# A third query buffer for a sparse graph-attention kernel, with its scatter, its tail and a table load moved

## The chip, the cores and the metric

The kernel runs on one core of a Trainium2 chip. The metric is the device time of one execution in microseconds. Six things work beside each other on the core: TensorE (matrix products; its weight loads are shown as a row of their own, PEld), VectorE (DVE), ScalarE (ACT), GpSimd (POOL, which here mostly issues indirect transfers), SyncE (SP, which issues plain transfers) and sixteen DMA engines.

## What is computed

The reference is one layer of graph attention over 3327 nodes with 1024 features, all in float32. Each node has few neighbours: an adjacency entry is set with a chance of 0.24%, made symmetric, and each node is its own neighbour.

```python
h = jnp.maximum(_layernorm(x, axis=-1), 0.0)
f = h @ Wf + bf
g = h @ Wg + bg
e = jax.nn.relu(f @ g.T)
scores = jnp.where(adj > 0, e, NEG)
attention = jax.nn.softmax(scores, axis=1)
x_W = h @ W + bW
x = x + attention @ x_W
```

Here `adj` is 3327 x 3327 and the three weights are 1024 x 1024.

## The kernel before

The kernel works on the edges only (`edge_path`); a dense path lies behind a branch that is taken only if a node has too many neighbours.

Two identities save most of the work. The score of an edge is h_i A h_j with A = Wf Wg^T, so that one vector q = h_i A per node suffices and no g is made. And the attention is summed over rows of h, y_i = sum of p_ij h_j, before it goes once through W.

**Part one**, to about 258 us, streams the adjacency matrix in 26 tiles of 128 rows, finds the column numbers of each row's edges, normalises x into `hd` in DRAM, makes A on TensorE, and sorts the nodes by degree. Each of 26 tiles of sorted nodes then has a fixed number of slots (`CAPS`, L27), 37 for the tile of the highest degrees and 11 for the last.

**Part two** runs over the tiles in the order `ORDER = [24, 0, 1, ... 23, 25]` (L29). The change is all in this part. For one tile s with cap slots:

- `fetch` (L733): GpSimd gathers the tile's edge lists (`pi`) and its own rows of h (into a buffer of the pool `G`).
- `prepare` (L748): TensorE transposes these rows (L703), ScalarE copies them to `hT` (L704), and TensorE makes q in three chunks of 342 columns, 24 products (L764). `prepared` (L786) and `emptied` (L776) copy the chunks from PSUM to the tile `q` (L780) and refill the emptied bank with the row that the next product adds to (L727).
- `dot` (L817): for each slot, GpSimd gathers 128 rows of 4 KB into a G buffer (L691), and VectorE takes their dot products with q (L824).
- `softmax` (L849): small operations on VectorE, one exponential on ScalarE (L860). Tiles of more than 16 slots are worked in two units, with the rescaling of an online softmax between them; smaller tiles are one unit. There are 15 tiles of two units in ORDER's middle (0 to 14).
- `combine` (L893): the weighted sum of the slots. `on_tensor` (L875) says which slots of the last unit TensorE adds: ScalarE scales such a row (L904) and TensorE adds it transposed into PSUM (L887, eight products a slot). The other slots are added by VectorE (L910) into the first row `y`, which ScalarE has scaled (L908). TensorE gets cap - 12 slots, in the last two tiles of ORDER cap - 7.
- `project` (L912): TensorE adds y transposed (L887), ScalarE copies the sum to `yT` (L918), TensorE multiplies it with W (L924, 16 products).
- `result` (L931): ScalarE copies the product out (L942), and GpSimd gathers the rows of x onto it with an accumulating transfer. `finish` (L951): GpSimd scatters the rows to `out` (L954).

The main loop (L1003) goes over the units. In the last unit of tile s it fetches and prepares the tile two places on, so that q is made two tiles ahead, and it holds two q. In front of the weighted sum, `AHEAD` = 3 dots of the next unit are placed. The scatter of an earlier result is placed in the next unit that comes, and has to wait there for the accumulating gather.

A scheduler orders the instructions of each engine at build time; `in_line` (L712) keeps the order of the products of TensorE and the copies of ScalarE as the program has it. Each engine then runs its own instructions in that fixed order. The pool `G` has 26 buffers; a gather waits for a free one.

Of the kernel before, what the change touches and what calls it, by code (L numbers as in the profile page):

```python
# [8 lines left out]
FP = mybir.dt.float32  # L9
I32 = mybir.dt.int32  # L10
AF = mybir.ActivationFunctionType
# [15 lines left out]
CAPS = [37, 25, 23, 22, 21, 21, 20, 20, 19, 19, 18, 18, 17, 17, 17, 16, 16, 15, 15, 15, 14, 14, 13, 13, 12, 11]  # L27

ORDER = [24, *range(24), 25]  # L29
ONE_CHUNK = 16  # L30
FIRST = 10
LARGEST = 16
AHEAD = 3
LAG = 4


# [259 lines left out]
def edge_path(ctx: ExitStack, tc: tile.TileContext, x, adj, Wf, bf, Wg, bg, W, bW, out, flag):  # L296
# [376 lines left out]

    bWb = ctx.enter_context(tc.tile_pool(name="bW", bufs=1)).tile([P, O], FP, name="bWb")
    nc.sync.dma_start(bWb, bW[None, :].to_broadcast([P, O]))
    psp = ctx.enter_context(tc.tile_pool(name="ps", bufs=3))
    gpool = ctx.enter_context(tc.tile_pool(name="G", bufs=26))
    mpool = ctx.enter_context(tc.tile_pool(name="more", bufs=1))
    qpool = ctx.enter_context(tc.tile_pool(name="q", bufs=2))
    hTpool = ctx.enter_context(tc.tile_pool(name="hT", bufs=1))  # L680
    yTpool = ctx.enter_context(tc.tile_pool(name="yT", bufs=1))
    xpool = ctx.enter_context(tc.tile_pool(name="xp", bufs=2))
    jpool = ctx.enter_context(tc.tile_pool(name="junk", bufs=1))
    small = ctx.enter_context(tc.tile_pool(name="small", bufs=2))
    p_q = ctx.enter_context(tc.tile_pool(name="p_q", bufs=2, space=PSUM))
    p_t = ctx.enter_context(tc.tile_pool(name="p_t", bufs=2, space=PSUM))
    p_y = ctx.enter_context(tc.tile_pool(name="p_y", bufs=1, space=PSUM))
# [33 lines left out]
    def filled(pool, name, row, w, at):  # L721
        ps = pool.tile([P, CB], FP, name=name)
        if at < 2:
            nc.tensor.matmul(ps, ident, A_sb[:, 0, :CB], start=True, stop=True)
        o = at * w % row.shape[1]
        banks[name, at] = ps
        return nc.scalar.copy(ps[:, :w], row[:, o : o + w])  # L727

    for at in range(2):
        filled(p_q, "ps_q", vb, QB, at)  # L730
# [2 lines left out]
    def fetch(s):  # L733

        if s == ORDER[1]:

            with tc.issue_after(st["gathered"].ins):
                return fetched(s)
        fetched(s)
# [8 lines left out]
    def prepare(s):  # L748
        e = st[s]
        pi = e["pi"]  # L750
        hT = hTpool.tile([P, KD, P], FP, name="hT")
        with in_line():
            copied, ins = transposed2(hT, e["hp"])
        if queue:
            queue["act"], queue["pe"] = copied, ins
        e["q"] = qpool.tile([P, QW], FP, name="q")
        e["ps_q"] = []
        for i, o in enumerate(range(0, QW, QB)):
            at = 3 * ORDER.index(s) + i
            ps = banks.pop(("ps_q", at))  # L760
            e["ps_q"].append(ps)
            with in_line():
                for k in range(KD):
                    ins = nc.tensor.matmul(  # L764
                        ps[:, :QB], hT[:, k, :], A_sb[:, k, o : o + QB], start=False, stop=(k == KD - 1),
                        skip_group_check=True,
                    )
            if queue:
                queue["pe"] = ins

            if not i:
                emptied(s, i)
        if not queue:
            prepared(s)
# [11 lines left out]
    def prepared(s):  # L786

        e = st[s]
        pi = e["pi"]
        emptied(s, 1)  # L790
        emptied(s, 2)
        df = pi.bitcast(FP)[:, KL : KL + 1]
        mask = e["mask"] = small.tile([P, KM], FP, name="mask")
        nc.vector.tensor_scalar(mask, iotak, df, NEG, op0=ALU.is_ge, op1=ALU.mult)
        e["sc"] = small.tile([P, KM], FP, name="sc")
        if s == NT - 1:
            e["x"] = gpool.tile([P, O], FP, name="G")
            gather(e["x"], x[:, :], perm[:, s : s + 1])
        e["edges"] = [pi[:, k : k + 1] for k in range(KL)]
        if s >= MORE:  # L800
            return

        ct = xpool.tile([P, O], FP, name="res")[:, : SEG * 8]
        with tc.issue_after(st["gathered"].ins):
            gather(ct, cd[:, :], perm[:, s : s + 1])
        found = mpool.tile([P, KM - KL + 8], FP, name="found")
        for i in range(0, KM - KL + 8, 8):
            nc.vector.max(found[:, i : i + 8], ct)
            if i < KM - KL:
                nc.vector.match_replace(ct, found[:, i : i + 8], ct, 0.0)  # L810
        more = mpool.tile([P, KM - KL], I32, name="more")
        nc.vector.tensor_scalar(more, found[:, 8:], 1.0, -1.0, op0=ALU.max, op1=ALU.add)
        e["edges"] += [more[:, k : k + 1] for k in range(KM - KL)]
# [61 lines left out]
    def on_tensor(s, k0, k1):  # L875


        m = min(max(0, CAPS[s] - (7 if s in ORDER[-2:] else 12)), k1 - k0 - 2) if s != ORDER[0] else (k1 - k0) // 2
        ks = range(max(k0, 1), k1)
        return [k for i, k in enumerate(ks) if (i + 1) * m // len(ks) > i * m // len(ks)]  # L880

# [11 lines left out]
    def combine(s, k0, k1, last):  # L893
        e = st[s]
        if not k0:
            e["y"] = G[s, 0]
        y = e["y"]
        e["first"] = True
        pe = on_tensor(s, k0, k1) if last else []
        for k in range(k0, k1):  # L900
            p = e["sc"][:, k : k + 1]
            g = G[s, k]
            if k in pe:
                queue["act"] = nc.scalar.activation(g, g, AF.Copy, scale=p)  # L904
                queue["pe"] = sum_transposed(e, g, e["first"], False)
                e["first"] = False
            elif k == 0:
                queue["act"] = nc.scalar.activation(y, y, AF.Copy, scale=p)  # L908
            else:
                e["summed"] = nc.vector.scalar_tensor_tensor(y, g, p, y, op0=ALU.mult, op1=ALU.add)  # L910
# [89 lines left out]


    rest, done_with = None, []
    for i, (s, k0, k1) in enumerate(units):  # L1003
        last = k1 == CAPS[s]
        at = ORDER.index(s)
        if last and at + 2 < NT:
            fetch(ORDER[at + 2])
        dots(s, range(k0, k1))
        softmax(s, k0, k1, last)
        if i + 1 < len(units):  # L1010
            s2, a, b = units[i + 1]
            dots(s2, range(a, min(b, a + AHEAD)))
        if done_with:
            finish(done_with.pop())
        combine(s, k0, k1, last)
        if rest:
            rest()
            rest = None
        if last:
            if at:  # L1020
                result(ORDER[at - 1])
                done_with.append(ORDER[at - 1])
            if at + 2 < NT:
                prepare(ORDER[at + 2])

            def rest(s=s, at=at):
                if at + 2 < NT:
                    prepared(ORDER[at + 2])
                project(s)

            if not at or i + 1 == len(units) or units[i + 1][2] == CAPS[units[i + 1][0]]:
                rest()
                rest = None
            if at + 2 == NT - 1:
                bad = failed()
# [43 lines left out]
```

## Time and profile before

| | |
|---|---|
| time, median of 3 | 1349.98 us (1345.41 to 1358.32) |
| profiled run | 1346.38 us, span 1344.7 us |
| TensorE busy | 1118.3 us, 83% |
| VectorE busy | 1166.1 us, 87% |
| ScalarE busy | 598.4 us, 44% |
| GpSimd busy | 901.1 us, 67% |
| data moved | 374.46 MB, mean 278 GB/s |
| GpSimd waiting in front of scatters for the gather of x | 66.4 us, 20 waits |
| ScalarE loads of an activation table | 3, 1283 ns each |

The profile is one execution on the chip. Busy time of an engine is what its instructions took; a wait is put down to the engine or transfer that came last. The chain of waits is followed back from the last instruction to what released each step, so it names what set the end. A table of stretches gives the same busy times for parts of the span, which is needed here because the limits change along it: about 258 us of part one, then tile 24 and the large tile 0 until 391 us, and then 25 tiles of falling size, at 31 to 55 us each.

### The profile page before, as it was taken

The page shows a single profiled execution, that of the slowest core. Times are in us where ns is not written, and L with a number is a line of the kernel's source. Part 1 is how long each engine was busy: PE and PEld are TensorE (multiplying, and loading weights), DVE is VectorE, ACT ScalarE, POOL GpSimd, SP SyncE. Part 2 cuts the span into 40 slices and gives each one's busy share as a digit, 9 for nine tenths or more (in the row PEclk, how much of TensorE's full clock was granted, in tenths as well). Part 3 has the DMA queues.
Part 4 walks back from the last instruction along what each step waited for, and adds up shares of the span by engine and source line. Part 5 has one row for each costly group of instructions (what it writes and reads, how often), then busy time and mean ns, then how long its engine had stood idle before and what let it go on. Part 6 is the DMA issues. An engine that isn't in the chain of part 4 may idle for free.

```text
span 1344.7 us, 14333 instructions
## 1 busy us (share of the span) xinstructions
PE 1118.3 (83%) x4448; PEld 707.6 (53%) x4448; DVE 1166.1 (87%) x2360; ACT 598.4 (44%) x940; POOL 901.1 (67%) x678
## 2 busy tenths in 40 slices
PE   2588896288339678989998999998999999999996
PEld 2355554155136546555565655555555555555553
DVE  4789899668978898999998999998988999999880
ACT  6779687223043534544354444433343333333250
POOL 6699889275566677677776666666665776766711
PEclk9989898598769899999998999999999999999998
DMA  9999996687569788898988879888786998888831
GB/s 355 336 381 348 385 382 206 249 306 270 169 201 315 249 285 304 275 307 288 309 298 299 281 279 309 308 292 298 235 278 210 295 288 284 284 272 265 293 100 50
DMA packets 101660, 374.46 MB, mean 278 GB/s; under 512 B 14731, under 2 KB 18474, under 8 KB 98247
## 3 DMA queue, kind: packets, MB, share of 16 engines
q0 software_dynamic: 79584, 286.77, 64.0%
q1 hardware_dynamic: 11004, 71.01, 13.7%
q10 hardware_dynamic: 10986, 15.67, 3.3%
q8 instruction: 37, 0.61, 0.2%
q14 instruction: 49, 0.40, 0.1%
HBM read 344.11 MB, written 29.30 MB: 278 GB/s over the span
## 4 chain that ended last, share of the span: by engine, by line
PE 46%; DVE 16%; issue 11%; ACT 10%; DMA 9%; POOL 6%; another core or an unknown queue 0%; ACTq 0%; POOLq 0%; SPq 0%; DVEq 0%
PE ps_o L924 19%; PE ps_q L764 17%; PE yT_ps L887 7%; ACT G L904 5%; DVE G L910 5%; DVE cand L478 4%; DMA G<-hd,pi 3%; DVE junk L824 3%; POOL G L691 3%; PE ps_A L554 2%; POOL r L427 2%; DMA r<-in_adj_dram 1%; ACT r L420 1%; DMA cd<-cand 1%; DMA hd<-xt 1%
## 5 line engine op out<-in xcount | busy, mean ns | idle before, releaser
L691 POOL DMA_INDIRECT G<-hd,pi x454 | 539.7, 1189 | 203.7 <-issue 109.5
L824 DVE CUSTOM_DVE_ANT_0 junk<-G,q 128x1024 bf16<-128x1024 f32 x456 | 584.9, 1283 | 58.2 <-DMA G<-hd,pi 30.5
L924 PE MATMUL ps_o<-W_sb,yT 128*128 128x512 f32 x832 | 370.3, 603 | 24.3 <-ACT yT L918 13.7
L764 PE MATMUL ps_q<-A_sb,hT 128*128 128x342 f32 x1248 | 371.5, 457 | 18.2 <-ACT hT L704 15.2
L910 DVE SCALAR_TENSOR_TENSOR G<-G,sc 128x1024 f32<-128x1024 f32 x279 | 357.8, 1282 | 14.1 <-ACT G L908 11.6
L764 PEld LDWEIGHTS ps_q<-A_sb,hT 128*128 128x128 f32 x1248 | 236.8, 192 | 144.8 <-ACT hT L704 20.6
L924 PEld LDWEIGHTS ps_o<-W_sb,yT 128*128 128x128 f32 x832 | 157.4, 192 | 221.8 <-issue 197.7
L887 PE MATMUL yT_ps<-ident,G 128*128 128x128 f32 x1512 | 188.6, 283 | 74.7 <-ACT G L904 66.1
L887 PEld LDWEIGHTS yT_ps<-ident,G 128*128 128x128 f32 x1512 | 177.1, 146 | 101.5 <-ACT G L904 74.6
L427 POOL TENSOR_TENSOR r<-r,iotaj 128x1664 f32<-128x1664 f32 (+3 forms) x52 | 191.4, 3711 | 29.7 <-ACT r L420 29.7
L904 ACT ACTIVATE G<-G,sc 128x1024 f32<-128x1024 f32 x163 | 173.1, 1135 | 47.2 <-DVE G L910 25.5
L780 ACT COPY q<-ps_q 128x342 f32<-128x342 f32 x78 | 34.8, 446 | 286.5 <-PE ps_q L764 256.1
L478 DVE MAX8 cand<-r 128x8 f32<-128x208 f32 (+2 forms) x416 | 121.8, 360 | 29.3 <-POOL r L427 29.3
L554 PE MATMUL ps_A<-WgT,WfT 128*128 128x342 f32 x432 | 138.0, 479 | 0.2 <-ACT WfT L535 0.2
L554 PEld LDWEIGHTS ps_A<-WgT,WfT 128*128 128x128 f32 x432 | 84.9, 201 | 59.6 <-issue 18.6
L420 ACT ACTIVATE r<-r 128x3327 f32<-128x3327 int32 (+4 forms) x28 | 77.8, 2779 | 1.4 <-ACT xt L464 0.5
L954 POOL DMA_INDIRECT out_dram<-res,perm x25 | 29.6, 1184 | 67.9 <-DMA res<-in_x_dram,perm 66.4
L691 POOL DMA_INDIRECT res<-in_x_dram,perm x25 | 44.3, 1773 | 36.2 <-ACT res L942 30.6
L860 ACT ACTIVATE sc<-sc,nm 128x10 f32<-128x10 f32 (+11 forms) x41 | 12.6, 308 | 109.0 <-DVE nm L857 91.4
L942 ACT COPY res<-ps_o 128x512 f32<-128x512 f32 x50 | 28.8, 576 | 68.1 <-PE ps_o L924 60.1
L691 POOL DMA_INDIRECT pi<-pd,perm x26 | 31.0, 1194 | 41.9 <-issue 39.9
L704 ACT COPY hT<-ps_t 128x512 f32<-128x512 f32 x52 | 28.1, 589 | 56.0 <-PE ps_t L703 44.7
(133 smaller groups left out, 684.4 us busy)
## 6 DMA issues: line engine op xcount, KB each, us to landing
r<-in_adj_dram SPq DMA_DIRECT2D x25, 1663.5 KB, 10.6
xt<-in_x_dram SPq DMA_DIRECT2D x25, 512.0 KB, 9.0
hd<-xt ACTq DMA_DIRECT2D x25, 512.0 KB, 8.2
G<-hd,pi POOLq DMA_INDIRECT x454
wr<-in_L_gnn_Wg_dram SPq DMA_DIRECT2D x8, 512.0 KB, 6.2
wr<-in_L_gnn_Wf_dram SPq DMA_DIRECT2D x8, 512.0 KB, 8.2
W_sb<-in_L_gnn_W_dram SPq DMA_DIRECT2D x1, 4096.0 KB, 17.8
cd<-cand ACTq DMA_DIRECT2D x25, 64.0 KB, 8.0
```

The source lines that it names most:

```text
L420: nc.scalar.activation(r[:n, b:e], a[:n, b:e], AF.Sign, accum_out=to)
L427: nc.gpsimd.tensor_mul(r[:n, b:e], r[:n, b:e], iotaj[:n, : e - b])
L478: nc.vector.max(cand[:n, s * 8 : s * 8 + 8], r[:n, s * SW : min(N, (s + 1) * SW)])
L554: nc.tensor.matmul(ps[:, :QB], WfTs[c][:, k, :], WgT[:, k, o : o + QB], start=(k == 0), stop=(k == KD - 1))
L691: return nc.gpsimd.indirect_dma_start(out=to, out_offset=None, in_=table, in_offset=bass.IndirectOffsetOnAxis(ap=idx, axis=0), **kw,)
L764: ins = nc.tensor.matmul(ps[:, :QB], hT[:, k, :], A_sb[:, k, o : o + QB], start=False, stop=(k == KD - 1), skip_group_check=True,)
L780: ins = nc.scalar.copy(e["q"][:, i * QB : (i + 1) * QB], e["ps_q"][i][:, :QB])
L824: nc.vector.tensor_tensor_reduce(junk, g, e["q"][:, :D], 1.0, e["q"][:, D : D + 1], op0=ALU.mult, op1=ALU.add, accum_out=e["sc"][:, k : k ...
L887: ins = nc.tensor.matmul(e["yT"][:, c, :], g[:, c * P : (c + 1) * P], ident, is_transpose=True, start=(first and c % 4 == 0), stop=(last a ...
L904: queue["act"] = nc.scalar.activation(g, g, AF.Copy, scale=p)
L910: e["summed"] = nc.vector.scalar_tensor_tensor(y, g, p, y, op0=ALU.mult, op1=ALU.add)
L924: ins = nc.tensor.matmul(ps, yT[:, k, :], W_sb[:, k, o * CB : (o + 1) * CB], start=False, stop=(k == KD - 1), skip_group_check=True,)
```

## The change

It keeps three q instead of two and makes q three tiles ahead. The third is made right behind the second one in the first pass of the loop, when TensorE would otherwise wait for tile 0. To make room the pool G goes from 26 to 25 buffers, and the pools of edge lists and of small tiles get one more. The rule that gives TensorE five slots more at the end now holds for the last three tiles of ORDER: tile 22 goes from 1 slot to 6. The scatter is placed only in the last unit of a tile, so that it doesn't stand in front of the gathers while x is still coming in. And one exponential of a single column is placed ahead of all, to load its table while ScalarE has nothing to do.

```diff
+QS = 3
...
-    psp = ctx.enter_context(tc.tile_pool(name="ps", bufs=3))
-    gpool = ctx.enter_context(tc.tile_pool(name="G", bufs=26))
+    psp = ctx.enter_context(tc.tile_pool(name="ps", bufs=4))
+    gpool = ctx.enter_context(tc.tile_pool(name="G", bufs=25))
...
-    qpool = ctx.enter_context(tc.tile_pool(name="q", bufs=2))
+    qpool = ctx.enter_context(tc.tile_pool(name="q", bufs=3))
...
-    small = ctx.enter_context(tc.tile_pool(name="small", bufs=2))
+    small = ctx.enter_context(tc.tile_pool(name="small", bufs=3))
...
+    one = small.tile([P, 1], FP, name="one")
+    nc.scalar.activation(one, ident[:, :1], AF.Exp)
...
-        m = min(max(0, CAPS[s] - (7 if s in ORDER[-2:] else 12)), k1 - k0 - 2) if s != ORDER[0] else (k1 - k0) // 2
+        m = min(max(0, CAPS[s] - (7 if s in ORDER[-QS:] else 12)), k1 - k0 - 2) if s != ORDER[0] else (k1 - k0) // 2
...
+    third = True
     for i, (s, k0, k1) in enumerate(units):
         last = k1 == CAPS[s]
         at = ORDER.index(s)
-        if last and at + 2 < NT:
-            fetch(ORDER[at + 2])
+        if last and at + QS < NT:
+            fetch(ORDER[at + QS])
         dots(s, range(k0, k1))
         softmax(s, k0, k1, last)
         if i + 1 < len(units):
             s2, a, b = units[i + 1]
             dots(s2, range(a, min(b, a + AHEAD)))
-        if done_with:
+        if done_with and last:
             finish(done_with.pop())
         combine(s, k0, k1, last)
+        if third:
+            third = False
+            fetch(ORDER[2])
+            prepare(ORDER[2])
+            prepared(ORDER[2])
         if rest:
             rest()
             rest = None
...
-            if at + 2 < NT:
-                prepare(ORDER[at + 2])
+            if at + QS < NT:
+                prepare(ORDER[at + QS])
 
             def rest(s=s, at=at):
-                if at + 2 < NT:
-                    prepared(ORDER[at + 2])
+                if at + QS < NT:
+                    prepared(ORDER[at + QS])
                 project(s)
```

## The prediction

> **What bounds the kernel now.** I read the page's busy times first, then the table of stretches, then the chain of waits, and last the timelines of single engines at the places that the change touches. Whole-span shares (TensorE 83%, VectorE 87%) say only that two engines are near their limit; the stretches say where each one is. From the table of stretches (time, then busy us and instructions of PE, PEld, DVE, ACT, POOL, then granted clock, DMA share, GB/s):
>
> ```profile
> 330.00:360.00 30.00, 16.88 (x47) 7.86 (x46) 29.75 (x43) 3.47 (x7) 14.65 (x9) 0.86 0.40 124
> 360.00:390.00 30.00, 0.00 (x0) 0.00 (x0) 27.49 (x44) 1.63 (x4) 19.50 (x11) 0.50 0.65 200
> 450.00:480.00 30.00, 29.04 (x167) 23.77 (x165) 21.97 (x34) 19.50 (x29) 20.40 (x17) 0.93 0.79 257
> 570.00:600.00 30.00, 28.72 (x138) 18.71 (x136) 29.08 (x45) 16.07 (x23) 22.74 (x21) 1.00 0.86 299
> 1000.00:1100.00 100.00, 97.26 (x371) 58.87 (x370) 91.02 (x132) 36.81 (x62) 67.69 (x52) 1.00 0.82 264
> 1100.00:1200.00 100.00, 97.26 (x356) 58.00 (x355) 96.05 (x137) 33.82 (x59) 71.06 (x58) 1.00 0.88 284
> ```
>
> The reader is to see three regimes. Tile 0 (300 to 391 us) is VectorE's: TensorE does nothing from 347 to 391. Tiles 1 to 7 (391 to about 725) are shared: VectorE is nearly full except for a few us at each tile boundary, and TensorE also idles some 40 us in all (the gaps of its timeline added up). From about 840 to the end TensorE is full; its remaining gaps (0.24 and 0.68 us a tile) are the waits for its own operand copies. The chain of waits agrees: it runs through VectorE and gathers before 725, and after that almost only through these:
>
> ```profile
> 464.75 7.62 DMA res<-in_x_dram,perm
> ...
> 476.19 5.74 DMA G<-hd,pi
> ...
> 1166.04 14.08 PE ps_q L764 x48
> 1181.66 14.00 PE ps_o L924 x32
> 1195.66 1.76 PE yT_ps L887 x16
> 1198.52 14.08 PE ps_q L764 x48
> ```
>
> So each late tile costs TensorE one q (14.07), one projection (14.00) and the transposes of its rows. The last lines I use are from the timeline: the table load, the first softmax of tile 0, and TensorE's tail (start us, us, engine, line, what; in brackets the idle time before and what ended it):
>
> ```profile
> 298.31 1.28 ACT L860 ACT_TABLE_LOAD   x1
> ...
> 331.85 1.03 PE L887 MATMUL yT_ps<-ident,G 128*128 128x128 f32 x8
> 332.92 1.07 ACT L918 COPY yT<-yT_ps 128x512 f32<-128x512 f32 x2
> ...
> 339.24 0.31 ACT L860 ACTIVATE sc<-sc,nm 128x19 f32<-128x19 f32 x1 [5.24 <-DVE nm L855]
> ...
> 341.69 1.28 DVE L910 SCALAR_TENSOR_TENSOR G<-G,sc 128x1024 f32<-128x1024 f32 x1
> ...
> 1292.06 6.27 PE L887 MATMUL yT_ps<-ident,G 128*128 128x128 f32 x56
> 1299.01 14.00 PE L924 MATMUL ps_o<-W_sb,yT 128*128 128x512 f32 x32 [0.68 <-ACT yT L918]
> ```
>
> [...] the softmax of tile 1's first 10 slots had its maximum at 405.2 us and ran on ScalarE only at 415.31, behind a copy that waited for q. [...] the load here is 1.28 us. [...] here a gather issued at 413.24 was used at 418.60, 5.4 us later[...].
>
> **The change, part by part.** Tile numbers follow ORDER, which is 24, 0, 1, ... 23, 25.
>
> *One q ahead.* The amount of work is the same; one q moves. Today TensorE makes tile 2's q at 409.5 to 423.6, after tile 0's transposes. In the changed instruction order it stands next to tile 1's q, before the first projection. TensorE idles 347 to 391, so the 15.3 us (8 transposes and a gap 1.28, then 14.07) are free on TensorE. From there on every tile still holds one q, two tiles become three ahead, and it is the end that has one fewer: before, q of tile 25 stands after tile 22's transposes (1262.6); after, one tile earlier. Removing it from the tail saves 8 transposes, 14.07 and the gap between, 1261.33 to 1276.51, about 15.2 us.
>
> *Five more slots of tile 22 on TensorE.* Only tile 22 is new (23 and 25 had it). It adds 5 x 8 transposes at 0.11 us (6.27 us for 56), 4.4 us on TensorE, and takes 5 x 1.28 = 6.4 us off VectorE and adds 5 x about 1.05 us on ScalarE, which is half idle. I worked the tail out from 1260.45, where the projection of tile 21 ends: transposes and wait 6.95 (1292.06 to 1299.01), projection 13.84, 6.95, 13.84, 5.2, 14.0, which gives 1321.2 instead of 1332.05. The tail gains 10.8 us. VectorE keeps up: its 6 remaining sums of tile 22, mixed with 3 dots, take some 11 us after a softmax that ends 3.5 us into the projection of tile 21, and the transposes need them 19 us in.
>
> *The price at tile 0.* The changed order puts the seven ScalarE copies of the extra q and its transposes ahead of the copies of tile 24's sum and of the softmax of tile 0's first 19 slots. Before, that softmax waited for VectorE alone (339.24). After, TensorE ends q of tile 1 at 331.85, q of tile 2 at 331.85 + 15.3 = 347.2, the last 8 transposes at 348.2; two copies to 349.4; softmax and the scaling of the first row (0.5 + 1.15) to 351.0. Behind it in VectorE's queue stands the first weighted sum; the changed order gives VectorE only one dot more before it (three after the maximum, not two), to 343.0. So VectorE stands still for 351.0 - 343.0 = 8.0 us, in a tile that it bounds alone, and everything after moves by that. The gathers wait too, since G buffers come free only with these sums. This is new and nothing hides it.
>
> *25 G buffers for 26.* At each boundary of tiles 1 to 5, VectorE waits for rows because gathers begin only when the last tile's slots come free, and GpSimd then issues one per 1.25 us. One buffer less is one row less in hand: 1.25 us each time. In tile 0 it makes 0.6.
>
> *Scatter only in last units.* In tiles 0 to 14 (two units) the scatter is issued about ten gathers later, when its rows have landed. GpSimd waits 66.4 us in 20 such waits (mean 3.3), but what VectorE feels is less: the long VectorE waits at the boundaries (3.66 at 418.60, 2.22 at 473.76, 2.58 at 522.86) are for rows gathered just before the scatter. Only the small waits after it (0.40 at 424.14; 0.38 and 0.30 at 479 to 482; 0.36 at 528) go away. The freed GpSimd time lets it catch up within three gathers, which returns part of the 1.25. Net for both edits I take +0.6 us in each of five boundaries, +3; bounds: -5 (all buffers' cost returned, and the large waits shortened) and +10 (1.25 in eight tiles).
>
> *Exponential table.* The order of ScalarE's instructions still has three loads before the second half: the first now is the exponential one, during the wait for the first rows (0.81 to 9.03), then the square root's, then the one in front of the softmax, as at 298.31. That one lies in a wait for VectorE (2.00 us idle after it). Nothing gained or lost.
>
> Four index buffers and three small ones cost only space. Sum: -10.8 + 8.0 + 0.6 + 3 = +0.8 us.
>
> **The rivals.** *First, faster:* the tail gain is whole and the stall at tile 0 is mostly absorbed, or the scatter's waits are worth more than I give them. For it: GpSimd's 66 us of waiting, 7.62 us of it on the chain at 464.75, and TensorE's loose gaps of some 11 us between 725 and 960, which a q in hand might close. Against it: VectorE was 99% busy from 330 to 360 and has no slack to absorb a stall with; no VectorE wait between 390 and 930 is for a q. Time: -10.8 + 2 - 3 = -12, about 1337. *Second, slower:* VectorE becomes the bound of the late tiles, so that the tail gain is not collected while stall and buffer loss are paid. For it: VectorE is 91 to 96% busy from 1000 to 1200, so an advance of 15 us uses up most of its 25 us of idle time after 840. Against it: 14.5 us of that idle time are waits for q, which disappear, and tile 22 gives it 6.4 more. Time: +8.6 + 6 - 3 = +12, about 1361. *Third, slower still:* 25 buffers starve VectorE by 1.25 us in fifteen tiles, on top of the stall: +8.6 + 19 - 10.8 = +17, 1366. Against it: late tiles hold 11 to 16 rows and their gathers are far ahead.
>
> **How the numbers follow.** The forecast has 0.50, the faster rival 0.30, the slower one 0.15, the third 0.05. The median before is 1349.98, but the profiled run, from which all this is worked, was 1346.38; I take the middle, 1348.2, plus 0.8: 1349. The range holds the forecast with the bounds of its buffer and scatter terms (-8 and +7) and the cores of the first two rivals: 1334 to 1362. Faster by over 1% means under about 1336, which is the better half of the first rival and a little more: 0.18. Slower by over 1% means over 1363: part of the second rival and the third, 0.12. Within: 0.70.
>
> **What would show it.** Right: a VectorE gap of about 8 us in front of a weighted sum near 343 to 351, released by ScalarE; TensorE busy with q through 347; yT transposes of tile 0 starting near 399 instead of 391; one q fewer after tile 21; the distance from the end of tile 21's projection to the end of the last one 60.8 us instead of 71.6; scatter waits of GpSimd far below 66 us. Wrong: no such gap, or transposes of tile 0 still at 391 (then the first rival); TensorE waiting for scaled rows by several us a tile after 1000 (then the second).

## The result, and the profile after

The changed kernel is slower: 1404.28 us (median of 6 runs, 1397.88 to 1405.31) against 1346.32 us for the kernel before beside it (1342.1 to 1358.32), a ratio of 1.0408 with a 95% interval of 1.0362 to 1.0454. Ratios and intervals in this document are estimated from all fast runs of both kernels (the few executions at least 1.5% above the fastest of the same kernel are left out) and not from the two medians, whose quotient is 1.0431 here. The forecast was 1349. The profiled run spans 1396.1 us. In the changed file lines stand one to five further down: the gather is L692, the dot L829, the exponential L865, the reciprocal L872, the scaling of the weights L875, the weighted sum L915, the transposes of the rows L892 and the projection L929.

The table of stretches again, for four of the windows of the prediction (us, busy us and instructions of PE, PEld, DVE, ACT, POOL, granted clock, DMA share, GB/s):

```profile
330.00:360.00 30.00, 28.67 (x104) 18.10 (x103) 16.39 (x28) 8.00 (x18) 1.90 (x2) 1.00 0.15 47
360.00:390.00 30.00, 9.45 (x23) 3.82 (x21) 25.21 (x31) 0.00 (x0) 16.07 (x13) 0.70 0.50 176
...
1000.00:1100.00 100.00, 90.46 (x345) 54.80 (x344) 83.97 (x122) 35.54 (x56) 60.35 (x48) 0.95 0.74 234
1100.00:1200.00 100.00, 89.73 (x299) 51.03 (x298) 83.94 (x121) 30.52 (x53) 60.36 (x52) 0.93 0.79 260
```

The first two rows show the price at tile 0 that was forecast: VectorE is down from 29.75 to 16.39 us while TensorE makes two q's. The last two rows show what was not forecast. From 1000 to 1200 us TensorE fell from 97 to 90%, VectorE from 91 to 96% down to 84%, GpSimd from 68 to 71% down to 60%, and the DMA share with them. No engine is as full there as TensorE was before, and the lines below show them waiting for each other. In the profile's chain of waits no engine has more than 19% of the span; before, PE led it with 46%. ("issue" is time in which the engine waited for nothing that the profile shows.)

```profile
DVE 19%; issue 19%; PE 13%; DMA 11%; POOL 6%; ACT 5%; POOLq 0%; DVEq 0%; ACTq 0%
```

Where the time went is read from the starts of the projections, tile by tile, on TensorE's timeline:

| stretch (start of projection to start of projection) | before | after |
|---|---|---|
| start of the span to tile 0 | 425.16 | 447.84 |
| tile 0 to tile 14 | 588.00 | 584.17 |
| tile 14 to tile 21 | 233.45 | 275.52 |
| tile 21 to the end of the last projection | 85.44 | 76.03 |

The start loses 22.7 us, the two-unit tiles win 3.8, the late one-unit tiles lose 42.1 and the tail wins 9.4. The win of 3.8 does not hold in general: on the quicker chips of the experiments the changed kernel takes 581.8 us for tiles 0 to 14, and two builds that are the kernel before as far as tile 14 (h1 and h2 below) take 572.3 and 573.7. The lines at the start and in the tail (start us, us, engine, line, what; in brackets the idle time before and what ended it):

```profile
298.22 1.28 ACT L865 ACT_TABLE_LOAD   x1
...
353.74 1.03 PE L892 MATMUL yT_ps<-ident,G 128*128 128x128 f32 x8
...
355.77 0.32 ACT L865 ACTIVATE sc<-sc,nm 128x19 f32<-128x19 f32 x1
...
357.40 1.28 DVE L915 SCALAR_TENSOR_TENSOR G<-G,sc 128x1024 f32<-128x1024 f32 x1 [12.30 <-ACT G L913]
...
1322.77 6.28 PE L892 MATMUL yT_ps<-ident,G 128*128 128x128 f32 x56
...
1329.72 14.00 PE L929 MATMUL ps_o<-W_sb,yT 128*128 128x512 f32 x32 [0.68 <-ACT yT L923]
```

The softmax of tile 0's 19 slots runs 16.5 us later than before (355.77 against 339.24) and the first weighted sum behind it waited 12.30 us for ScalarE. The tail after tile 21's projection is one q shorter, as forecast: 1322.77 to 1383.55 is 60.8 us.

Now one late tile in the changed kernel, tile 16 with 16 slots. All lines are from the timeline:

```profile
1070.58 1.97 PE L892 MATMUL yT_ps<-ident,G 128*128 128x128 f32 x8 [5.90 <-DVE G L915]
...
1073.22 16.49 PE L929 MATMUL ps_o<-W_sb,yT 128*128 128x512 f32 x32 [0.68 <-ACT yT L923]
...
1073.55 0.32 ACT L865 ACTIVATE sc<-sc,nm 128x16 f32<-128x16 f32 x1
...
1078.58 1.28 DVE L829 CUSTOM_DVE_ANT_0 junk<-G,q 128x1024 bf16<-128x1024 f32 x1 [2.68 <-DMA G<-hd,pi]
...
1079.79 0.16 DVE L872 RECIPROCAL rs<-l 128x1 f32<-128x1 f32 x1
...
1080.26 1.15 ACT L913 ACTIVATE G<-G,sc 128x1024 f32<-128x1024 f32 x1 [6.30 <-DVE sc L875]
...
1083.19 1.74 POOL L692 DMA_INDIRECT G<-hd,pi  x1 [5.23 <-DVE G L915]
```

In this excerpt the projection is that of tile 15; the exponential, the reciprocal and the sums are those of tile 16. The exponential, with the read-out of its sum, was done at 1073.96. The reciprocal that needs it, an operation of 0.16 us, ran at 1079.79, because four dots of the *next* tile stand ahead of it in VectorE's fixed order, and the last of these had to wait 2.68 us for its row. ScalarE then stood 6.30 us for the scaled weights, no weighted sum ran meanwhile, no buffer of G came free, and GpSimd stood 5.23 us. The next rows came later for that, and TensorE, whose last eight transposes of a tile need the finished sum, waited 5.90 us in the tile before and 3.10 in this one. The same place in the kernel before, at the projection of tile 16:

```profile
1079.90 1.03 PE L887 MATMUL yT_ps<-ident,G 128*128 128x128 f32 x8
...
1083.12 0.16 DVE L867 RECIPROCAL rs<-l 128x1 f32<-128x1 f32 x1
...
1084.71 1.15 ACT L908 ACTIVATE G<-G,sc 128x1024 f32<-128x1024 f32 x1 [2.37 <-DVE sc L870]
```

There the transposes did not wait, and the reciprocal ran 0.78 us behind its exponential, which was done at 1082.34.

The seven gaps of TensorE of this kind ahead of tiles 15 to 21 (5.90, 3.10, 4.25, 0.41, 5.20, 1.92, 3.42) add up to 24.2 us. The projections behind them took 16.49, 16.93, 17.03, 14.00, 16.25, 16.22 and 15.40 instead of 14.00, 14.3 us more, and the eight transposes ahead of each 1.09 to 1.97 instead of 1.04, 3.8 us. That is 42.3 us, the whole loss of the late tiles. The granted clock beside these times is in the last section.

### The profile page after: what moved, and what is told of

Same layout as the page of the kernel before. It is cut to its first block, busy times and chain, and to the rows that moved or that the text cites. A ratio compares the mean times of both kernels' runs of the same rounds, so it can differ in the third digit from the quotient of the medians.

```text
span 1396.1 us, 14400 instructions
## 1 busy us (share of the span) xinstructions
PE 1145.4 (82%) x4488; PEld 718.8 (51%) x4488; DVE 1157.8 (83%) x2355; ACT 603.4 (43%) x946; POOL 904.5 (65%) x678
## 4 chain that ended last, share of the span: by engine, by line
DVE 19%; issue 19%; PE 13%; DMA 11%; POOL 6%; ACT 5%; POOLq 0%; DVEq 0%; ACTq 0%
DVE G L915 11%; DMA G<-hd,pi 10%; PE ps_o L929 7%; DVE junk L829 7%; POOL G L692 5%; ACT G L909 4%; PE ps_q L769 3%; PE yT_ps L892 3%; DVE sc L829 1%; DMA G<-hd,more 1%; POOL pi L692 0%; ACT G L877 0%; ACT yT L923 0%; PE ps_t L704 0%; ACT ps_o L728 0%
## 5 line engine op out<-in xcount | busy, mean ns | idle before, releaser
L692 POOL DMA_INDIRECT G<-hd,pi x454 | 556.0, 1225 | 310.2 <-DVE G L915 147.5
L829 DVE CUSTOM_DVE_ANT_0 junk<-G,q 128x1024 bf16<-128x1024 f32 x456 | 583.8, 1280 | 110.1 <-DMA G<-hd,pi 99.6
L929 PE MATMUL ps_o<-W_sb,yT 128*128 128x512 f32 x832 | 380.0, 616 | 20.5 <-ACT yT L923 18.4
L769 PE MATMUL ps_q<-A_sb,hT 128*128 128x342 f32 x1248 | 374.5, 460 | 25.0 <-issue 17.1
L915 DVE SCALAR_TENSOR_TENSOR G<-G,sc 128x1024 f32<-128x1024 f32 x274 | 351.1, 1281 | 20.3 <-ACT G L913 17.9
L892 PE MATMUL yT_ps<-ident,G 128*128 128x128 f32 x1552 | 198.1, 286 | 99.7 <-ACT G L909 75.5
L929 PEld LDWEIGHTS ps_o<-W_sb,yT 128*128 128x128 f32 x832 | 160.9, 196 | 224.6 <-issue 199.5
L892 PEld LDWEIGHTS yT_ps<-ident,G 128*128 128x128 f32 x1552 | 182.1, 147 | 131.4 <-ACT G L909 89.2
L428 POOL TENSOR_TENSOR r<-r,iotaj 128x1664 f32<-128x1664 f32 (+3 forms) x52 | 191.3, 3716 | 32.5 <-ACT r L421 32.5
L909 ACT ACTIVATE G<-G,sc 128x1024 f32<-128x1024 f32 x168 | 178.3, 1136 | 71.8 <-DVE sc L875 66.9
L785 ACT COPY q<-ps_q 128x342 f32<-128x342 f32 x78 | 34.7, 444 | 278.7 <-PE ps_q L769 236.2
L865 ACT ACTIVATE sc<-sc,nm 128x10 f32<-128x10 f32 (+11 forms) x41 | 12.6, 307 | 127.5 <-DVE nm L862 120.6
L692 POOL DMA_INDIRECT res<-in_x_dram,perm x25 | 41.8, 1674 | 22.3 <-ACT res L947 15.3
L692 POOL DMA_INDIRECT pi<-pd,perm x26 | 29.3, 1128 | 37.9 <-issue 34.8
L913 ACT ACTIVATE G<-G,sc 128x1024 f32<-128x1024 f32 x26 | 29.9, 1148 | 43.4 <-DVE sc L875 42.9
```

The source lines that it names most:

```text
L428: nc.gpsimd.tensor_mul(r[:n, b:e], r[:n, b:e], iotaj[:n, : e - b])
L692: return nc.gpsimd.indirect_dma_start(out=to, out_offset=None, in_=table, in_offset=bass.IndirectOffsetOnAxis(ap=idx, axis=0), **kw,)
L769: ins = nc.tensor.matmul(ps[:, :QB], hT[:, k, :], A_sb[:, k, o : o + QB], start=False, stop=(k == KD - 1), skip_group_check=True,)
L785: ins = nc.scalar.copy(e["q"][:, i * QB : (i + 1) * QB], e["ps_q"][i][:, :QB])
L829: nc.vector.tensor_tensor_reduce(junk, g, e["q"][:, :D], 1.0, e["q"][:, D : D + 1], op0=ALU.mult, op1=ALU.add, accum_out=e["sc"][:, k : k ...
L892: ins = nc.tensor.matmul(e["yT"][:, c, :], g[:, c * P : (c + 1) * P], ident, is_transpose=True, start=(first and c % 4 == 0), stop=(last a ...
```

## The experiments

Two theories stood against each other for the late tiles. *Order*: dots of the next tile stand ahead of the reciprocal. Counted in the order of VectorE's instructions in the traces, from the softmax's mask operation to its reciprocal in tiles 15 to 21, there are two of them in the kernel before and four to seven in the changed one. *Starvation*: 25 buffers are one too few. Beside them stood questions on the start, the scatter and the buffer by itself. Each ratio is to runs of the kernel before on the same chip; because chips differ, that took 1325 to 1327 us beside the runs of the upper part of the table and 1354 beside the four of the lower part (b_again, g1, f3_late_order, g3_late_order), so ratios are compared within a chip speed. Expectations that are given in us were written for a kernel before of 1346 us and are read as ratios to it.

| run | ratio, 95% interval | tiles 0 to 14 | 14 to 21 | 21 to end |
|---|---|---|---|---|
| after_again (changed kernel) | 1.0474 (1.0440 to 1.0507) | 581.8 | 276.8 | 76.5 |
| e1_g25 | 1.0146 (1.0100 to 1.0191) | 586.2 | 239.2 | 85.4 |
| f4_q2lead | 1.0115 (1.0085 to 1.0146) | 577.4 | 234.2 | 89.8 |
| f1_order | 1.0093 (1.0061 to 1.0126) | 578.0 | 233.5 | 74.6 |
| f6_after_four | 1.0271 (1.0240 to 1.0302) | 582.1 | 254.8 | 74.6 |
| f2_late | 1.0387 (1.0344 to 1.0430) | 579.1 | 278.8 | 76.8 |
| f3_again | 1.0014 (1.0004 to 1.0025) | 575.4 | 233.4 | 74.6 |
| g3_again | 0.9921 (0.9900 to 0.9943) | 569.0 | 233.5 | 74.6 |
| f5_late_order_oldscatter | 1.0112 (1.0093 to 1.0130) | 586.6 | 233.4 | 74.6 |
| e3_scatter | 0.9965 (0.9952 to 0.9977) | 565.1 | 233.5 | 85.4 |
| h1_before_order | 1.0122 (1.0099 to 1.0145) | 572.3 | 250.6 | 85.4 |
| h2_before_order6 | 1.0240 (1.0215 to 1.0265) | 573.7 | 262.8 | 85.4 |
| h3_before_order6_g25 | 1.0437 (1.0412 to 1.0462) | 583.0 | 266.0 | 92.4 |
| *beside before at 1354:* b_again | 1.0015 (0.9983 to 1.0047) | 584.5 | 236.2 | 85.7 |
| g1_after_g26 | 1.0312 (1.0233 to 1.0391) | 580.3 | 279.7 | 76.3 |
| f3_late_order | 0.9933 (0.9910 to 0.9956) | 585.1 | 236.6 | 74.6 |
| g3_late_order_g26 | 0.9944 (0.9913 to 0.9974) | 579.7 | 237.6 | 74.6 |

The three right-hand columns are us of the profiled run between starts of projections, as in the table above. Where nothing disturbs the late tiles, 14 to 21 take 233.4 to 233.5 us on the quicker chips, with two q's or three (234.2 in f4_q2lead).

### One buffer less, in the kernel before (e1_g25)

```diff
-    gpool = ctx.enter_context(tc.tile_pool(name="G", bufs=26))
+    gpool = ctx.enter_context(tc.tile_pool(name="G", bufs=25))
```

> The kernel before with one edit: 25 row buffers instead of 26. Everything else, the order of VectorE's instructions in the late tiles included, stays as before. Theory A (order of VectorE): the 40 to 45 us that tiles 15 to 21 lose in the changed kernel come from the next tile's products that stand ahead of the softmax's reciprocal, so one buffer less costs little here: 1346 to 1354 us. Theory B (starvation): 25 buffers are too few for the late tiles, so they lose the same 40 us with the old order: 1380 to 1395 us.

The ratio of 1.0146 is 19 us of 1325 (the medians, 1347.97 and 1325.17, lie 23 apart). As ratios the two ranges are 1.000 to 1.006 and 1.025 to 1.036, and the run lies in neither. Starvation would have put the 40 us into the late tiles, and these lost 5.7 (239.2). But the buffer is not as cheap as the order theory had it. Most of its price lies ahead of tile 7. Against h1 and h2 below, tile 0's projection starts 3.6 and 6.3 us later, tiles 0 to 7 take 12 to 14 us more (329.3 against 315.5 and 317.1), and tiles 7 to 14 the same (256.9 against 256.8 and 256.6). From 425 to 1000 us VectorE waits 31.2 us for rows here and 18.3 and 20.7 there.

### The order mended in the changed kernel (f1_order, f6_after_four)

```diff
-                dot(s, k, st[ORDER[-2]].get("summed") if s == ORDER[-1] else None)
+                behind = st[ORDER[-2]].get("summed") if s == ORDER[-1] else None
+                at = ORDER.index(s)
+                if not behind and k >= 2 and at > 1 and CAPS[s] <= ONE_CHUNK:
+                    behind = st[ORDER[at - 1]].get("scaled")
+                dot(s, k, behind)
```

`scaled` is the instruction of L875. In f6_after_four the 2 is a 4.

> The changed kernel with one edit: in the tiles of one unit, every product of the next tile but the first two has to stand behind the scaling of the softmax's weights of the tile at hand, so VectorE runs max, mask, one or two products, reciprocal, scaling as it did before the change. 25 buffers and the third q stay. Theory A: most of the loss of the late tiles goes, 1404 - 40 = 1364 us (1355 to 1375). Theory B: the rows are missing whatever the order, 1395 to 1405 us.

> The changed kernel with at most four products of the next tile ahead of the reciprocal in the late tiles (the planner's own order has five to seven, the run with the order mended two). If the number ahead sets the loss: four cost 17 us in the kernel before, so tiles 14 to 21 take 233 + 17 = 250 us, ratio 1.0093 + 17/1325 = 1.022 (1.016 to 1.028). Rival (any product beyond the second costs, since with 25 buffers there is no slack): 265 us or more, ratio 1.033 or more.

With two dots ahead the late tiles are back at 233.5 us, to a tenth what they took before the change, with 25 buffers and the third q still there. The ratio falls from 1.0474 to 1.0093, some 50 us, into the range of the order theory (1.006 to 1.021 as ratios). The same place in this run's timeline, with the projection of tile 16 and the softmax of tile 17:

```profile
1080.83 1.04 PE L892 MATMUL yT_ps<-ident,G 128*128 128x128 f32 x8
...
1082.54 14.00 PE L929 MATMUL ps_o<-W_sb,yT 128*128 128x512 f32 x32 [0.68 <-ACT yT L923]
...
1083.30 0.16 DVE L872 RECIPROCAL rs<-l 128x1 f32<-128x1 f32 x1 [0.63 <-ACT sc L865]
...
1083.77 1.15 ACT L913 ACTIVATE G<-G,sc 128x1024 f32<-128x1024 f32 x1 [0.50 <-DVE sc L875]
```

The reciprocal now waits for its exponential, not for a dot, and the sums start half a us after it. The table of waits, from 1000 to 1300 us (engine and line, what it waited for: us, times, longest), of the kernel before:

```profile
POOL G L691 <- DVE G L910: 27.8, 29, 4.8
...
DVE junk L824 <- ACT q L780: 14.5, 7, 6.5
...
ACT G L908 <- DVE sc L870: 11.8, 5, 2.4
```

of the changed kernel:

```profile
POOL G L692 <- DVE G L915: 81.4, 39, 8.6
...
DVE junk L829 <- DMA G<-hd,pi: 46.2, 39, 3.9
ACT G L913 <- DVE sc L875: 34.4, 7, 7.0
...
PE yT_ps L892 <- DVE G L915: 20.4, 5, 5.9
```

and of f1_order, where TensorE's wait for the sums is gone altogether:

```profile
POOL G L692 <- DVE G L915: 26.4, 38, 2.3
...
ACT G L913 <- DVE sc L875: 5.9, 10, 1.2
DVE junk L829 <- DMA G<-hd,pi: 1.3, 2, 0.9
```

VectorE's 46.2 us of waits for rows, which looked like too few buffers, are 1.3 us with the same 25 buffers: they were a consequence. With four ahead the loss is 254.8 - 233.5 = 21.3 us, near the 17 expected, and the ratio of 1.0271 is in the range given for that. So the loss follows the number of dots ahead: none with two, 21 us with four, 42 with the four to seven of the changed kernel.

### The order alone, in the kernel before (h1, h2, h3)

```diff
-            nc.vector.reciprocal(rs, l)
+            with tc.issue_after(ahead().ins) if ahead else ExitStack():
+                nc.vector.reciprocal(rs, l)
...
+        late = at > 1 and i + 1 < len(units) and CAPS[s] <= ONE_CHUNK
+
+        def ahead():
+            s2, a, b = units[i + 1]
+            dots(s2, range(a, a + 4))
+            return st[s2]["dotted"]
```

`dotted` is the last dot so far, and `ahead` is handed to `softmax` in the tiles that are `late`; h2 and h3 have 6 for 4, and h3 has 25 buffers as well. Two q's and the old scatter stay.

> The kernel before (26 row buffers, two q's ahead, old scatter) with one edit: in the tiles of one unit the softmax's reciprocal has to stand behind the fourth product of the next tile, as it does in the changed kernel. Theory A (the order of VectorE is the cause by itself): tiles 15 to 20 take 36 to 40 us instead of 33, so 6 or 7 tiles by 4 to 6 us = 25 to 42 us: ratio 1.019 to 1.031. Theory C (the order hurts only together with the third q, whose row takes one more slot and whose copies stand in ScalarE's queue): 1.000 to 1.008, late tiles at 33 to 34 us.

> The kernel before (26 buffers, two q's, old scatter) with the reciprocal of the late tiles behind the sixth product of the next tile instead of the fourth. The changed kernel's own order has five to seven ahead of it there. Theory D (each product ahead of the reciprocal beyond the rows that are already there makes the reciprocal wait for a gather, whose slot comes free only by the sums behind the last reciprocal): the loss in tiles 15 to 21 grows from 17 us with four to 35 to 45 us: ratio 1.025 to 1.034. Rival (the third q or the buffer makes up the rest of the 42 us): 1.010 to 1.016, as with four.

> The kernel before with the reciprocal of the late tiles behind the sixth product of the next tile and 25 row buffers instead of 26; still two q's, old scatter. With 26 buffers tiles 14 to 21 lost 29 us, in the changed kernel 43. Theory E (one slot less makes the sixth product wait for one more sum): the loss there grows to 40 us or more, ratio 1.024 + 0.0146 + 0.008 = 1.045 or so (1.040 to 1.052). Rival (the third q makes the rest): the loss there stays at 29 us, ratio 1.024 + 0.0146 = 1.039 (1.034 to 1.041).

Order alone makes the kernel before slower, with none of the change's own edits in it. (GpSimd's order changes with it, from 980 us on; ScalarE's stays as it was.) Four dots cost 17.1 us in tiles 14 to 21, less than the 25 to 42 that I had expected. Six cost 29.3, again less than the 35 to 45 expected, and the ratio of 1.0240 lies just under its range. Six with 25 buffers cost 32.5 there and 7.0 more behind tile 21, and the ratio of 1.0437 is in the range in which the buffer adds to the loss. So the loss grows with the dots ahead, and a missing buffer makes it larger, 10 us here. From h2's table of waits (1000 to 1300 us; its L911 is the weighted sum, L871 the scaling):

```profile
POOL G L691 <- DVE G L911: 72.3, 25, 10.1
...
ACT G L909 <- DVE sc L871: 61.6, 9, 7.7
DVE junk L824 <- DMA G<-hd,pi: 31.7, 17, 5.6
```

One correction comes from here. Theory D said that the reciprocal waits for a gather. In h2 none of the six dots in tiles 15 to 21 waits for its row. The reciprocal is late by the dots themselves: it runs 4.6 to 7.0 us behind its exponential, and the waits for rows come after it, because buffers come free later. In the changed kernel there is both: the reciprocal runs 2.4 to 6.6 us behind the exponential, and the dots ahead of it wait 15.1 us for rows in these seven tiles. With what is lost behind tile 21 counted in, h3 loses 39.5 us and the changed kernel 43.5 and 45.3 (its two profiles, against builds with the mended order). That rest of 4 to 6 us is not explained.

### 26 buffers in the changed kernel (g1_after_g26)

```diff
-    gpool = ctx.enter_context(tc.tile_pool(name="G", bufs=25))
+    gpool = ctx.enter_context(tc.tile_pool(name="G", bufs=26))
...
-    bWb = ctx.enter_context(tc.tile_pool(name="bW", bufs=1)).tile([P, O], FP, name="bWb")
-    nc.sync.dma_start(bWb, bW[None, :].to_broadcast([P, O]))
+    bWb = ctx.enter_context(tc.tile_pool(name="bW", bufs=1)).tile([P, O], BF, name="bWb")
+    nc.gpsimd.dma_start(bWb, bW[None, :].to_broadcast([P, O]))
```

> The changed kernel with 26 row buffers instead of 25; the space comes from the bias, which is kept in bf16 instead of fp32. The order of VectorE in the late tiles stays as in the changed kernel: three to five products ahead of the reciprocal. Theory A (order is the cause, one buffer a cost of its own of 1.5%, as with 25 buffers in the kernel before): 1.041 - 0.015 = 1.026 (1.020 to 1.032), and tiles 15 to 20 still take 36 to 40 us each. Theory C (the order hurts only because the 26th buffer is missing): the late tiles return to 32.5 to 34 us and the ratio falls to 1.000 to 1.010.

The space for the buffer comes from the bias, which is kept in bf16. Still slow, 279.7 us for tiles 14 to 21: one buffer doesn't cure it, and the ratio of 1.0312 is in the range of the order theory. In this build five to eight dots stand ahead of the reciprocal, one more than with 25. The scheduler seems to pull the next tile's dots forward as far as buffers allow, once q is three ahead; in all builds with two q's ahead and no edit of the order (e1, f4, e3) there are two. Why it does so is not shown. What the traces do show is that in the kernel before the dots of the next tile waited for their q (14.5 us in the table of waits above), and that with three q's no such wait is left there: the late q may have been what held the dots back.

### Two q's ahead, all else changed (f4_q2lead)

```diff
-QS = 3
+QS = 2
...
-            fetch(ORDER[2])
-            prepare(ORDER[2])
-            prepared(ORDER[2])
+            pass
```

The five slots stay with the last three tiles.

> The changed kernel with q's made two tiles ahead instead of three; all pools keep the sizes of the changed kernel (25 row buffers, 3 q buffers), the scatter, the early table load and the five slots stay. The order of VectorE in the late tiles is then as before the change. Theory A (order): the late tiles run as before, no start to pay, the tail as before: 1346 to 1358 us. Theory B (25 buffers starve): 1380 to 1395 us, with the start's 15 to 20 us off from 1404 and the late tiles' loss kept.

The late tiles are whole (234.2), with 25 buffers, which the starvation theory did not allow for. The ratio, 1.0115, is a little above the order theory's range (1.000 to 1.009); it has the buffer's price in it. The tail is 4.4 us longer than before (89.8 against 85.4), which is the five slots' price on TensorE to the tenth, without the q that pays for it.

### The start (f2_late, f3_late_order, f3_again)

```diff
-        if third:
+        if third and i == 1:
             third = False
-            fetch(ORDER[2])
-            prepare(ORDER[2])
-            prepared(ORDER[2])
+            fetch(ORDER[3])
+            prepare(ORDER[3])
+            prepared(ORDER[3])
```

and in the first pass of the loop ORDER[2] where the changed kernel has ORDER[3]. The two f3 runs have the mended order too.

> The changed kernel with the extra q made one unit later, behind the first 19 slots of tile 0, instead of ahead of them and of the first projection. Theory of the start: the 22.7 us that the changed kernel is behind at tile 0's transposes are the two q's that stand in the queues ahead of tile 0's softmax (14 to 17 us of TensorE each); one of them moved gives back about 14 us there. The late tiles keep their order and 25 buffers. If the backlog of the start reaches the end: 1404 - 14 = 1390 us. Rival: the late tiles are bound by VectorE's waits for rows, and the lead that is gained early on is given back before tile 15, because a later start only empties the reserve of q's: 1400 to 1405 us.

> The changed kernel with both edits: the extra q made behind the first 19 slots of tile 0, and the next tile's products behind the scaling of the weights in the late tiles; 25 buffers. With the late tiles bound by TensorE again, what is won at the start should reach the end: in the run with the late q alone tile 14's projection began 7 us earlier than in the run with the order alone, so 1.009 - 7/1325 = 1.004 (1.000 to 1.006). Rival (the start's backlog is regained before tile 15 anyway, because three q's of lead let TensorE catch up): 1.008 to 1.011.

> The changed kernel with the extra q made behind tile 0's first slots and the next tile's products behind the scaling, 25 buffers; 0.9933 beside a slow run of the kernel before, 1.0112 for the same kernel with the old scatter beside a quick one. If the scatter is worth 0.35% here as in the kernel before, and the buffer's 15 us in the middle tiles (0 to 14) are paid only where the kernel before is quick: 1.008 on a chip where the kernel before takes 1325, 0.993 where it takes 1354. Rival (the scatter is worth 1.8% once three q's are ahead): 0.993 on either.

The transposes of tile 0 on TensorE, first in f1_order (extra q ahead of tile 0), then in f2_late (behind), then in f4_q2lead (none), all with 25 buffers on the same chip:

```profile
402.14 16.70 PE L892 MATMUL yT_ps<-ident,G 128*128 128x128 f32 x128 [44.02 <-ACT G L909]
```

```profile
394.16 16.81 PE L892 MATMUL yT_ps<-ident,G 128*128 128x128 f32 x128 [36.99 <-ACT G L909]
```

```profile
392.99 16.70 PE L892 MATMUL yT_ps<-ident,G 128*128 128x128 f32 x128 [50.36 <-ACT G L909]
```

The extra q costs 8.0 us against f2 and 9.2 against f4. The 22.7 us of the first profile hold more than that: its copies of tile 1's rows to hT had waited 5.37 and 2.95 us with no releaser that the profile names, and a repeat of the kernel before (b_again) shows such a wait of 11.17 us at the same copies. Such waits of ScalarE, over 1.5 us between 255 and 420 us, stand in all six traces of runs beside a kernel before of 1346 or 1354 us and in none of the thirteen beside 1325 to 1327. So they were seen on the slower chips alone; their cause stays open. By time, moving the q takes the changed kernel from 1.0474 to 1.0387 and the mended one from 1.0093 to 1.0014, 10 to 12 us, so a backlog made at tile 0 does reach the end. The expectations missed the sizes: f2's 1.0387 lies between its two ranges (1.033, and 1.040 to 1.044), and f3 is outside both of its ranges beside either speed (0.9933 and 1.0014).

### The scatter (e3, f5) and the buffer beside three q's (g3)

```diff
-        if done_with:
+        if done_with and last:
             finish(done_with.pop())
```

e3 is the kernel before with this alone; f5 is f3 without it; the g3 runs are f3 with 26 buffers.

> The kernel before with the scatter alone moved into the last units; 26 buffers, two q's ahead. From the run with two q's ahead (ratio 1.0115, with the 4.4 us of tile 22's slots in it) and the one with 25 buffers alone (1.0146): 1.0115 - 0.0033 - 0.0146 = -0.0064, so 0.994 (0.990 to 0.998): GpSimd no longer holds gathers behind the 66 us of waits for results. Rival: the waits were hidden, 0.998 to 1.002.

> As the run with both edits (extra q late, products behind the scaling, 25 buffers: 0.9933), with the scatter in every unit as before the change. If the scatter's move is worth 0.6% here too: 0.999 (0.996 to 1.003). Rival (nothing): 0.991 to 0.996.

> As the run with both edits, with 26 row buffers (bias in bf16). If the buffer is worth the 1.5% that it was worth in the kernel before: 1.004 - 0.015 = 0.989 (0.984 to 0.994), and the 11 us of the tail are then all that is left. Rival (the buffer's price is paid only where two q's of lead leave TensorE nothing else to do, and the third q covers it): 1.000 to 1.005, no better than with 25.

> The same with 26 row buffers (bias in bf16). Where the kernel before takes 1325 us, the 26th buffer should be worth what it is worth there, 1.0146 - 1 = 1.5%: 1.008 - 0.015 = 0.993 (0.988 to 0.998). Rival (with three q's ahead the buffer is worth nothing, as beside the slow run of before): equal to the run with 25, within 0.3%.

The scatter alone is worth 0.35%, 4.6 us: about 8 in tiles 0 to 14 by the trace (565.1 against 572.3 and 573.7), inside the expected range and short of its middle, 0.994. f5 missed both of its ranges, since they started from f3's 0.9933 beside a kernel before of 1354. Beside 1326 f3 has 1.0014, and the scatter is then worth 1.0% with three q's, 11 us of it in tiles 0 to 14. The 26th buffer is worth 0.9% there (g3_again, as expected). Beside 1354 its worth is not resolved: the ratios show nothing (0.9944 against 0.9933, outside both ranges of g3_late_order_g26), the medians of the runs, 1342.73 and 1347.33, 0.3%.

g3, with the mended order, the late q, the scatter, the tail and 26 buffers, was faster than before on both chips, 0.9921 and 0.9944. It keeps the bias in bf16, which was not run alone. The kernel before with the scatter alone has 0.9965 and needs nothing of the kind.

> The kernel before, unchanged, so that its trace can be laid beside the others on the same chip: ratio 0.997 to 1.003 to itself. Every theory expects the same.

> The changed kernel, unchanged, beside the same runs of the kernel before as the three below: ratio 1.035 to 1.050, as first measured. It is here because the absolute times of the kernel before differ by 2% between the chips of the earlier runs (1325, 1346 and 1354 us), so that ratios of different calls can't be subtracted to less than 1%.

Both came out as expected.

## Why the prediction was wrong

The terms that it had were right in direction, and all but one near in size. The step that failed is that it put the late tiles at nothing: it did not ask what the order of VectorE does to them.

- *Tail, -10.8 us: right.* 21 to the end took 74.62 us in every run with a mended order, against 85.44, so 10.8; in the changed kernel itself 1.4 less, since tile 21's projection ran slow behind a gap.
- *Price at tile 0, +8.0 us: right*, 8.0 and 9.2 by the traces. The mechanism, ScalarE's copies for the extra q ahead of tile 0's softmax, is what the profile shows. The gap of VectorE that it forecast at 8 us is 12.30 in the first profile, with the unexplained waits in it, and 5.75 to 6.43 in the three others with the extra q ahead of tile 0 on the quicker chips.
- *Buffer and scatter, +3.6 us with bounds of -5 and +10: the buffer mis-sized.* Counted alone it is +19 us and the scatter -4.6. The step "one buffer less is one row less in hand: 1.25 us each time" counted five boundaries; the buffer was missed at the start (4 to 6 us), in tiles 0 to 7 (12 to 14) and in the late tiles (5.7). That the third rival has 19 us for it too is luck: it has them in fifteen equal shares, and tiles 7 to 14 lost nothing.
- *Table load, 0: the loads were three again*, the last one at 298.22 as before.
- *Scatter waits of GpSimd far below 66 us: right*, 20.3 us in 5 waits.
- *Late tiles, not in the sum: 42.1 us.* The part "The change part by part" read the changed instruction order at tile 0 and named there that VectorE gets one dot more ahead of the first sum. It did not read that order in the one-unit tiles, where two to five dots more stand ahead of the reciprocal. Its third rival was put aside with "late tiles hold 11 to 16 rows and their gathers are far ahead": they were far ahead only as long as sums freed buffers in time. With the order mended and the same 25 buffers the 42 us are gone (f1), and with four or six dots ahead the kernel before, otherwise unchanged, loses 17 or 29 us there (h1, h2).

The sign that the prediction gave for its second rival, TensorE waiting several us a tile after 1000, came true, but not for that rival's reason. VectorE did not become the bound; it was less busy than before. The terms measured one by one, -10.8, +8 to 9, +19, -4.6 and +42 to 43, add up to about +55 us, in which the buffer's 5.7 us in the late tiles are counted twice: +49 without them. The measured change is +58 on the first chip and +64 on the quicker one, so 9 to 15 us are not assigned; in the first profile the two unexplained waits at the start, 8.3 us, are among them. The order is the largest part: mending it took some 50 of the 64 us away, and six dots ahead, alone in the kernel before, cost 2.4%, or 32 us.

The step at tile 0 rested on the order of ScalarE's instructions. The late tiles show the same on VectorE: a reciprocal whose input was ready at 1073.96 ran at 1079.79, behind the four dots that stand ahead of it in VectorE's order.

## What to carry to other kernels

When a change alters how far ahead work may be placed, read the new order of every engine in every stage, and ask of each short operation that others wait for (a reciprocal, a scaling of weights) how much long work now stands ahead of it. A wait for rows is not yet a want of buffers: look at what holds the buffers, and move that first. Where all engines' shares fall together in a stage, as here from 1000 us on, look for a loop of waits: no busy time names its cause.

## What the runs showed of the hardware

Six of the seven gaps of TensorE cost more than themselves. Behind the gap of 5.90 us eight transposes took 1.97 us instead of 1.04, and the projection 16.49 instead of 14.00; the granted clock was 0.50 from 1068.1 to 1078.2 us, some 10 us that begin inside the gap, and 1.00 from there to 1090. Around the gap of 3.10 us it was 0.50 for some 7 us (1112.5 to 1119.2), with 1.14 us for the transposes and 16.93 for the projection. The gap of 1.92 us was followed by 1.83 and 16.22. Behind that of 0.41 us the clock stayed at 1.00 up to 1206, with 1.09 and 14.00. The seven gaps, 24.2 us in all, so became a loss of 42. The line of the shortest gap that was followed by a clock of 0.50, and that clock (time, PE busy, granted clock, DMA share, GB/s):

```profile
1265.82 1.83 PE L892 MATMUL yT_ps<-ident,G 128*128 128x128 f32 x8 [1.92 <-DVE G L915]
...
1266.10:1272.80 6.70, 6.03 (x14) 0.50 0.91 349
```

The kernel before took 1325 to 1327 us on some chips, 1346 on one and 1354 on another. Tiles 0 to 14 then took 572 to 588 us (h1 and h2 stand for the kernel before on the quicker chips), while tiles 14 to 21 differed by 3 us at most. A ratio of 1% there holds only for runs beside each other.
